# Layer 0's depthwise convolution split between VectorE and TensorE, and zeros only in the border cells of layer 1's table

## The chip, the cores and the metric

The kernel runs on one core of one Trainium2 chip. Time is the device time of one execution, in microseconds (us). In all that follows PE is TensorE (PEld its weight loads), DVE is VectorE, ACT is ScalarE, POOL is GpSimd and SP is SyncE, which only issues transfers here. All data is fp32 unless said otherwise.

## What is computed

The reference is a network of four layers on an input x of 2 images, 64 x 64 positions and 128 channels. Only its first two steps concern the change:

```
# layer 0, for each image: x = x + f(groupnorm(x)), and f begins
xz   = h @ W_in.T                   # 128 -> 512: 256 channels xs, 256 channels z
xs   = silu(depthwise_conv3x3(xs))  # each channel with nine weights of its own, zero padding
...                                 # four selective scans over xs, layernorm, gate silu(z), W_out
# layer 1: x = x + deformable_conv3x3(groupnorm(x))
#   reads the image at computed positions, four neighbours each; outside the image a neighbour counts as 0
```

Layer 2 (a selective scan with 512 channels and 256 states, then spectral filters) and layer 3 (attention, then a mixture of experts) are unchanged and follow after that.

## The kernel before, in words

The input X (128 partitions x 64 tiles x 128 channels, 4.2 MB) is loaded whole with eight transfers of 512 KB on SP's queue (`move`, L1353). Before that, `zero_table` fills layer 1's table with zeros by one transfer on POOL's queue (L437). The table lies in DRAM: for each of the two images 67 x 67 cells of 512 values (2 KB), 18.4 MB in all. A cell holds the values of four neighbouring positions, so that layer 1 can fetch all four with one gather (L534). Layer 1 itself writes the cells that belong to image positions with sixteen transfers (L480), long after layer 0.

`layer0` goes through the two images one after the other, and each image through three blocks:

- The block before the scan. The 32 tiles of the image are transposed to channels on partitions (`to_channels`, L95, copies L72 and L74, into xt, 128 x 4096). `groupnorm` takes statistics on DVE (L132, L133), sums them over groups of channels by matmuls with the constant gmat (pm L136, pq L143; gmat is loaded on SP's queue behind X, L200), and normalises xt in place (L146). Then PE forms z (pz, L209, 16 matmuls), ACT applies Silu and SP stores z to DRAM (L211, L212). For each half h of the 256 channels, PE forms px (L221, 8 matmuls of 128 x 512), which DVE and ACT copy in turn into the middle of xp, a tile of 66 x 66 with a frame of zeros. The convolution is done on PE: for each of eight pieces q of 8 image rows, nine matmuls (L227) of the diagonal matrix `dw[:, h * 9 + t]` with the shifted window of xp are added up in PSUM (pc), and ACT writes Silu of it to U (L228). The 18 diagonal matrices are products of the identity with a column of weights, made by DVE (L215).
- The scan (L255 to L394), an order written out by hand. It begins with copies of U to uc (L255).
- The block after the scan: layernorm, gate, W_out, and the sum onto X (L403 to L425).

Outside the scan a scheduler orders the instructions of each engine by their dependences; an engine then works through its own list in that order. Constants of layer 0 (w_xp L170, w_dt L172, w_out L179; sel L175 and L177, mean_w L181, an L183 and L184, dd L187) are loaded or made within the first block of the first image. PSUM has six buffers for the tiles of the first block, and the working pool `wk` has three of each of its tiles.

Of the kernel before, what the change touches and what calls it, by code (L numbers as in the profile page):

```python
# [16 lines left out]
F32 = mybir.dt.float32  # L17
# [3 lines left out]
ALU = mybir.AluOpType  # L21
# [4 lines left out]
P = 128  # L26
B, HH, WW, C = 2, 64, 64, 128
# [13 lines left out]
TS = 67  # L41
# [48 lines left out]
def to_channels(k, ps, out, tile_of, n):  # L90

    for g in range(0, n, 4):
        pt = ps.tile([P, N], F32, name="pt", tag="ps")
        for j in range(4):
            k.nc.tensor.transpose(pt[:, j * P : (j + 1) * P], tile_of(g + j), k.ident)  # L95
        k.copy(out[:, g * P : (g + 4) * P], pt)
# [29 lines left out]
def groupnorm(k, pool, ps, gmat, xt, tag):  # L126

    nc = k.nc
    st = pool.tile([P, 8, 6], F32, name=f"{tag}_st", tag=f"{tag}_st")
    mv = pool.tile([P, 2], F32, name=f"{tag}_mv", tag=f"{tag}_mv")  # L130
    for i in range(8):
        nc.vector.bn_stats(st[:, i, :], xt[:, i * N : (i + 1) * N])  # L132
    nc.vector.bn_aggr(mv, st.rearrange("p a b -> p (a b)"))  # L133
    mg = pool.tile([P, 1], F32, name=f"{tag}_mg", tag=f"{tag}_mg")
    pm = ps.tile([P, N], F32, name="pm", tag="ps")
    nc.tensor.matmul(pm[:, 0:1], gmat, mv[:, 0:1], start=True, stop=True)  # L136
    nc.vector.tensor_copy(mg, pm[:, 0:1])
    q = pool.tile([P, 1], F32, name=f"{tag}_q", tag=f"{tag}_q")
    nc.vector.tensor_tensor(q, mv[:, 0:1], mg, ALU.subtract)
    nc.vector.tensor_tensor(q, q, q, ALU.mult)  # L140
    nc.vector.tensor_tensor(q, q, mv[:, 1:2], ALU.add)
    pq = ps.tile([P, N], F32, name="pq", tag="ps")
    nc.tensor.matmul(pq[:, 0:1], gmat, q, start=True, stop=True)  # L143
    rs = pool.tile([P, 1], F32, name=f"{tag}_rs", tag=f"{tag}_rs")
    rsqrt(nc, pool, rs, pq[:, 0:1], 1e-5, [P, 1], tag)
    nc.vector.tensor_scalar(xt, xt, mg, rs, ALU.subtract, ALU.mult)  # L146


def zero_frame(nc, t):

    nc.gpsimd.memset(t[:, 0, :], 0.0)
    nc.gpsimd.memset(t[:, 65, :], 0.0)
    nc.gpsimd.memset(t[:, 1:65, 0:1], 0.0)
    nc.gpsimd.memset(t[:, 1:65, 65:66], 0.0)
# [4 lines left out]
def layer0(k):  # L159
    tc, nc, ins, X = k.tc, k.nc, k.ins, k.X  # L160
    T = N
    NC = L // T
    with ExitStack() as es:
# [29 lines left out]
        for b in range(B):  # L193
            Xb = X[:, b * NTB : (b + 1) * NTB, :]
            with ExitStack() as e2:
                pre = e2.enter_context(tc.tile_pool(name=f"l0p{b}", bufs=1))
                wk = e2.enter_context(tc.tile_pool(name=f"l0w{b}", bufs=3))
                ps = e2.enter_context(tc.tile_pool(name=f"l0ps{b}", bufs=6, space=PSUM))
                gmat = pre.tile([P, P], F32, name="gmat")
                nc.sync.dma_start(out=gmat, in_=ins["gmat"])  # L200
                w_in = pre.tile([P, 512], F32, name="w_in")
                nc.sync.dma_start(out=w_in, in_=ins["w_in0"])
                xt = pre.tile([P, L], F32, name="xt")
                to_channels(k, ps, xt, lambda i: Xb[:, i, :], NTB)
                groupnorm(k, pre, ps, gmat, xt, "gn")
                for h in range(2):
                    for q in range(8):
                        pz = ps.tile([P, N], F32, name="pz", tag="ps")
                        nc.tensor.matmul(pz, w_in[:, 256 + h * P : 256 + (h + 1) * P], xt[:, q * N : (q + 1) * N], start=True, stop=True)  # L209
                        z = wk.tile([P, N], F32, name="z")  # L210
                        nc.scalar.activation(z, pz, AF.Silu)  # L211
                        nc.sync.dma_start(out=zs[h, :, b * L + q * N : b * L + (q + 1) * N], in_=z)  # L212
                dw = pre.tile([P, 18, P], F32, name="dw")
                for j in range(18):
                    nc.vector.tensor_scalar(dw[:, j, :], k.ident, k.v("conv_w")[:, j : j + 1], None, ALU.mult)  # L215
                for h in range(2):
                    xp = pre.tile([P, 66, 66], F32, name="xp", bufs=2)
                    zero_frame(nc, xp)
                    for q in range(8):
                        px = ps.tile([P, N], F32, name="px", tag="ps")  # L220
                        nc.tensor.matmul(px, w_in[:, h * P : (h + 1) * P], xt[:, q * N : (q + 1) * N], start=True, stop=True)  # L221
                        k.copy(xp[:, 1 + 8 * q : 9 + 8 * q, 1:65], px.rearrange("p (h w) -> p h w", w=WW))
                    for q in range(8):
                        pc = ps.tile([P, N], F32, name="pc", tag="ps")
                        for t in range(9):
                            ky, kx = divmod(t, 3)
                            nc.tensor.matmul(pc, dw[:, h * 9 + t, :], xp[:, 8 * q + ky : 8 * q + ky + 8, kx : kx + WW], start=t == 0, stop=t == 8)  # L227
                        nc.scalar.activation(U[:, h, q * N : (q + 1) * N], pc, AF.Silu, bias=k.v("conv_b")[:, h : h + 1])  # L228

            with ExitStack() as e2:  # L230
                ch = e2.enter_context(tc.tile_pool(name=f"l0h{b}", bufs=2))
                sm = e2.enter_context(tc.tile_pool(name=f"l0s{b}", bufs=1))
                wk = e2.enter_context(tc.tile_pool(name=f"l0k{b}", bufs=3))
# [77 lines left out]
                at = lambda i: (todo[i][0], NC - 1 - todo[i][1] if todo[i][0] >= 2 else todo[i][1])  # L311
# [4 lines left out]
                def spread(bc, q):  # L316
                    br = wk.tile([P, 4, T], F32, name="br", bufs=2)
                    nc.sync.dma_start(out=br, in_=bc[4 * q : 4 * q + 4, :].partition_broadcast(P))
                    return br

                def c_row(cs, n):
                    o = pc_.tile([P, T], F32, name="pcn")
                    nc.tensor.matmul(o, sel[:, n, :], cs, start=True, stop=True)  # L323
                    return o
# [13 lines left out]
                with tc.manual_schedule():  # L338
                    rows, pcn, last, save = spread(ready[0][1], 0), c_row(ready[0][2], 0), None, None
                    for it, (kk, ci) in enumerate(todo):  # L340
                        c = at(it)[1]
                        uc, bc, cs, dt, du, ea = ready.pop()
                        f = T - 1 if kk >= 2 else 0
# [6 lines left out]
                        for n in range(16):  # L350
# [13 lines left out]
                            flat, dflat = (t.rearrange("p h t -> p (h t)")[:, s_] for t in (S, dA))  # L364
# [23 lines left out]
                            if n % 4 == 2:  # L388
                                if n < 14:
                                    rows = spread(bc, n // 4 + 1)  # L390
                                elif ready:
                                    rows = spread(ready[0][1], 0)
# [4 lines left out]
            with ExitStack() as e2:  # L397
                wk = e2.enter_context(tc.tile_pool(name=f"l0f{b}", bufs=2))
# [30 lines left out]

def zero_table(k, pool, table):  # L430

    nc = k.nc
    row = B * TS * 4
    z = pool.tile([P, row], F32, name="zero")
    nc.gpsimd.memset(z, 0.0)
    flat = table.rearrange("a c -> (a c)").rearrange("(p g f) -> p g f", p=P, f=row)
    nc.gpsimd.dma_start(out=flat, in_=z.unsqueeze(1).to_broadcast([P, TS, row]))  # L437


def layer1(k, table):  # L440
# [915 lines left out]
def kernel(tc, ins, out, stages=STAGES):  # L1356
    nc = tc.nc
    with ExitStack() as es:
# [8 lines left out]
        if two or "0" in stages or "1" in stages:  # L1367
            with tc.tile_pool(name="x01", bufs=1) as xp:
                k.X = xp.tile([P, NT, C], F32, name="X")
                move(nc, k.X, tokens(x))  # L1370
                if "1" in stages:
                    table = dr.tile([B * TS * TS, 4 * C], F32, name="table")
                    with tc.tile_pool(name="zt", bufs=1) as zp:
                        zero_table(k, zp, table)
                if "0" in stages:
                    layer0(k)
                with ExitStack() as e2:
                    if two:
                        mix = mixing_weights(k, dr, e2)
                    if "1" in stages:  # L1380
                        layer1(k, table)
                    if two:
                        weights = mix()
                if two:
                    norm_tokens(k, rs, sh)
                x = dr.tile([B * L, C], F32, name="x1")
                move(nc, tokens(x), k.X)
# [119 lines left out]
```

## Time and profile before

| | |
|---|---|
| median of 3 runs | 16111.0 us (16098.64 to 16113.83) |
| the profiled execution | 16122.4 us, its span 16120.6 us |
| mean granted TensorE clock | 0.902 |
| busy share of the span | PE 76%, PEld 45%, DVE 86%, ACT 61%, POOL 84% |
| first matmul of the convolution, image 1 and 2 | 92.25 us and about 2402 us |
| last Silu of the convolution, image 1 and 2 | 222.93 us and 2533.5 us |
| layer 1: first table store, first gather | 4700.6 us and 4873.8 us |

The profiled execution is one execution on the chip. A line of the profile's groups gives the source line, engine, operation, and output and inputs by the names of the program, then the count, and after the bar the busy time in us, the mean duration of one in ns, and the idle time of the engine just before them with what ended it. Each fp32 matmul appears as two records, one for each pass. A line of waits gives who waited for whom, the total in us, how often, and the longest. A line of windows gives the stretch in us, its length, the busy time and number of instructions of each engine, the granted TensorE clock as a share of full speed, the mean busy share of the 16 DMA engines, and the GB/s moved. A line of the timeline gives the start in us, the time to the end of the last of the instructions merged in it, and their number.

### The profile page before, as it was taken

The numbers are of one execution on the slowest core, as the hardware profiler recorded it, in microseconds if no ns is written. First come the engines' busy times: TensorE is split into PE (matmuls) and PEld (weight loads), VectorE is DVE, ScalarE is ACT, GpSimd is POOL, SyncE is SP. The second block draws the span as 40 slices with busy tenths as digits, with TensorE's granted clock in tenths as the row PEclk, the third lists the DMA queues.
The fourth block names the chain that finished last, engine by engine and source line by source line (L and its number), as shares of the span: only waits on it lengthen the run. The fifth ranks groups of instructions, "written<-read, shape, count | busy, mean of one in ns | idle before, by whom it ended". The sixth has DMA issues, their size and how long they took to land.

```text
span 16120.6 us, 190989 instructions
## 1 busy us (share of the span) xinstructions
PE 12236.8 (76%) x69886; PEld 7246.4 (45%) x69886; DVE 13783.2 (86%) x12003; ACT 9835.0 (61%) x15912; POOL 13463.0 (84%) x5125
## 2 busy tenths in 40 slices
PE   6666657666667864549778679879788888888897
PEld 2222223222227851325445446546445555555565
DVE  4999975999964359999999999999999999999973
ACT  3666634666610027777777677777777777777752
POOL 3888835888817879999999999999999999999970
PEclk8999989999988876769889889989999999999998
DMA  2111111111135544546555556556666665565543
GB/s 102 69 71 69 68 51 49 70 71 69 69 93 160 160 143 151 168 150 203 183 187 195 174 181 199 193 184 203 192 193 198 189 204 195 190 205 194 188 169 128
DMA packets 1214859, 2389.69 MB, mean 148 GB/s; under 512 B 346648, under 2 KB 923288, under 8 KB 1047904
## 3 DMA queue, kind: packets, MB, share of 16 engines
q1 hardware_dynamic: 1162672, 2206.74, 41.7%
q0 software_dynamic: 50384, 169.42, 3.5%
q8 instruction: 552, 9.04, 0.2%
q14 instruction: 387, 3.17, 0.1%
q10 hardware_dynamic: 864, 1.32, 0.0%
HBM read 2018.49 MB, written 358.65 MB: 147 GB/s over the span
## 4 chain that ended last, share of the span: by engine, by line
POOL 34%; PE 13%; DVE 10%; DMA 3%; ACT 2%; issue 1%; SPq 0%; POOLq 0%; ACTq 0%; DVEq 0%
POOL S L1082 33%; DVE S L1138 10%; PE pef L966 6%; PE Z L1100 2%; PE acc L939 2%; DMA row<-drow 2%; PE pw L765 1%; POOL S L1088 1%; ACT ze L1106 1%; ACT dA L1136 0%; DMA w<-in_w_b_dram 0%; DMA w<-in_w_delta_dram 0%; ACT e L946 0%; PE acc L1001 0%; DMA e<-mdr 0%
## 5 line engine op out<-in xcount | busy, mean ns | idle before, releaser
L1138 DVE TENSOR_TENSOR_SCAN S<-dA,S 128x512 f32<-128x512 f32 x8192 | 9226.5, 1200 | 393.0 <-ACT dA L1136 208.4
L1082 POOL TENSOR_TENSOR S<-row,g 128x4096 f32<-128x4096 f32 x1024 | 9103.0, 8895 | 256.3 <-DMA row<-drow 219.8
L1136 ACT ACTIVATE dA<-row,a_t 128x512 f32<-128x512 f32 x8192 | 5614.4, 692 | 2146.0 <-DVE S L1138 2107.7
L1100 PE MATMUL Z<-S,cv 128*32 128x256 f32 x32768 | 2499.4, 435 | 1494.0 <-ACT ze L1106 1240.3
L966 PE MATMUL pef<-hk,ur 128*128 128x256 f32 x14336 | 3512.1, 388 | 138.8 <-ACT e L946 120.0
L966 PEld LDWEIGHTS pef<-hk,ur 128*128 128x128 f32 x14336 | 2644.6, 191 | 1077.6 <-issue 563.4
L365 DVE TENSOR_TENSOR_SCAN S<-dA,S 128x1024 f32<-128x1024 f32 x1024 | 2339.1, 2284 | 243.7 <-ACT dA L363 96.8
L354 POOL TENSOR_TENSOR S<-du,br 128x1024 f32<-128x1024 f32 x1024 | 2410.3, 2357 | 138.6 <-DVE M L379 83.3
L1100 PEld LDWEIGHTS Z<-S,cv 128*32 128x32 f32 x32768 | 999.9, 121 | 2698.6 <-issue 1289.2
L394 PE MATMUL yp<-M,ident 128*128 128x512 f32 x4096 | 2062.6, 627 | 2.9 <-DVE M L379 2.9
L394 PEld LDWEIGHTS yp<-M,ident 128*128 128x128 f32 x4096 | 821.7, 201 | 2091.7 <-issue 2052.7
L363 ACT ACTIVATE dA<-dt,an 128x511 f32<-128x511 f32 x2048 | 1406.9, 687 | 209.0 <-DVE S L365 132.0
L379 DVE TENSOR_TENSOR M<-S,pcn 128x1024 f32<-128x1024 f32 x1024 | 1250.5, 1221 | 110.5 <-DVE S L365 6.9
L323 PE MATMUL pcn<-cs,sel 80*128 80x512 bf16 x1024 | 409.3, 400 | 1180.4 <-DVE M L379 1169.8
L1106 ACT COPY ze<-Z 128x512 f32<-128x512 f32 x1024 | 1122.4, 1096 | 235.0 <-PE Z L1100 201.2
L939 PE MATMUL acc<-e,mw 128*128 128x512 f32 x1920 | 1042.2, 631 | 29.1 <-ACT e L946 28.5
L534 POOL DMA_INDIRECT G<-table,idx x576 | 802.2, 1393 | 261.1 <-issue 175.1
L966 PEld LDWEIGHTS pef<-hd,ur 128*128 128x128 f32 x4096 | 761.4, 195 | 491.7 <-issue 233.0
L966 PE MATMUL pef<-hd,ur 128*128 128x256 f32 (+1 forms) x4096 | 882.0, 342 | 99.8 <-ACT e L946 93.8
L541 DVE TENSOR_TENSOR V<-G,wt 128x4608 f32<-128x4608 f32 x64 | 317.5, 4962 | 609.0 <-DMA G<-table,idx 590.9
L367 ACT COPY stt<-S 128x2 f32<-128x2 f32 x896 | 168.9, 189 | 1083.5 <-DVE S L365 1080.3
L553 PE MATMUL pv<-ident,V 128*128 128x128 f32 x4608 | 615.3, 302 | 52.1 <-issue 48.8
(323 smaller groups left out, 8302.1 us busy)
## 6 DMA issues: line engine op xcount, KB each, us to landing
row<-drow SPq DMA_DIRECT2D x1024, 1024.0 KB
br<-bc SPq DMA_DIRECT2D x256, 1024.0 KB
zd<-ze SPq DMA_DIRECT2D x1024, 256.0 KB
hk<-in_phi_dram SPq DMA_DIRECT2D x128, 576.5 KB
hk<-in_phi_dram SPq DMA_DIRECT2D x96, 704.5 KB
hd<-in_phi_dram SPq DMA_DIRECT2D x512, 128.5 KB
mw<-wdr SPq DMA_DIRECT2D x480, 128.0 KB
hk<-in_phi_dram SPq DMA_DIRECT2D x160, 320.5 KB
```

The source lines that it names most:

```text
L354: nc.gpsimd.tensor_tensor(S, du, br[:, n % 4, :].unsqueeze(1).to_broadcast([P, 2, T]), ALU.mult)
L363: nc.scalar.activation(dA[:, h, rest], dt[:, h, rest], AF.Exp, scale=an[:, kk * 2 + h, n : n + 1])
L365: nc.vector.tensor_tensor_scan(flat, dflat, flat, 0.0, ALU.mult, ALU.add)
L379: nc.vector.tensor_tensor(M, S, pcn.unsqueeze(1).to_broadcast([P, 2, T]), ALU.mult)
L394: nc.tensor.matmul(yp[:, h, :], k.ident, M[:, h, :], start=False, stop=n == 15)
L939: nc.tensor.matmul(acc.rearrange("p a s -> p (a s)"), ms[f][:, o, :], e, start=box["first"], stop="whole" in box and (f, o) == todo[-1])
L966: nc.tensor.matmul(pe[:, a, 256 - n :], ur[:, par, j, :], h[:, at : at + n], start=i == 0, stop=i + 1 == len(mm))
L1082: nc.gpsimd.tensor_tensor(S, row.unsqueeze(1).to_broadcast([P, 2, R, T]), g.unsqueeze(2).to_broadcast([P, 2, R, T]), ALU.mult)
L1100: nc.tensor.matmul(Z[32 * j : 32 * j + 32, q], cv[:, h, s], S[:, h, :, s], start=h == 0, stop=h == 1)
L1106: nc.scalar.copy(ze.rearrange("p q t e -> p q e t"), Z)
L1136: nc.scalar.activation(dA, row[:, j % R, :], AF.Exp, scale=a_t[:, h, d : d + 1])
L1138: nc.vector.tensor_tensor_scan(s, dA, s, 0.0, ALU.mult, ALU.add)
```

## The change

The convolution's nine taps are divided. Taps 0, 1 and 2 (the upper row of the 3 x 3 window) stay as matmuls with diagonal matrices. Taps 3 to 8 are added up by DVE in a tile sv: one tensor_scalar (window times weight), then five scalar_tensor_tensor (window times weight, plus sv, in place). PE adds sv to pc by a matmul with the identity. So PE does four matmuls for a piece q instead of nine, and DVE six instructions that it did not have. Only six diagonal matrices per image are left, and POOL makes them. The tile dw shrinks from 18 to 6 matrices of 512 bytes per partition; three buffers of sv, 2 KB per partition each, are added.

`zero_table` now writes zeros only where layer 1 writes no or not all values of a cell: for each image the first two and last two rows of cells (two transfers of 2 x 67 cells), and in between, for each row, the last two cells together with the first two of the next row (one transfer of 64 pieces of 8 KB). These are six transfers, 2.15 MB in all, instead of one of 18.4 MB.

The scheduler's lists differ only around these parts: in DVE's list the sv instructions of neighbouring pieces q are interleaved, and the making of sel, mean_w, an and dd stands before the first copies of px; in ACT's list the exponential for an stands before the first z, one table load less is needed, and three of the first four copies to uc stand before the last Silu of the convolution; in SP's list w_xp, w_dt and w_out stand before the stores of z; in POOL's list three of the products dw stand between the first four and the last two transfers of zeros, the other three after them.

```diff
@@ layer0
-                dw = pre.tile([P, 18, P], F32, name="dw")
-                for j in range(18):
-                    nc.vector.tensor_scalar(dw[:, j, :], k.ident, k.v("conv_w")[:, j : j + 1], None, ALU.mult)
+                KT = 3
+                dw = pre.tile([P, 2, KT, P], F32, name="dw")
+                for h in range(2):
+                    for t in range(KT):
+                        nc.gpsimd.tensor_scalar(dw[:, h, t, :], k.ident, k.v("conv_w")[:, h * 9 + t : h * 9 + t + 1], None, ALU.mult)
...
                     for q in range(8):
+                        tap = lambda t: xp[:, 8 * q + t // 3 : 8 * q + t // 3 + 8, t % 3 : t % 3 + WW]
+                        cw = lambda t: k.v("conv_w")[:, h * 9 + t : h * 9 + t + 1]
+                        sv = wk.tile([P, 8, WW], F32, name="sv")
+                        nc.vector.tensor_scalar(sv, tap(KT), cw(KT), None, ALU.mult)
+                        for t in range(KT + 1, 9):
+                            nc.vector.scalar_tensor_tensor(sv, tap(t), cw(t), sv, ALU.mult, ALU.add)
                         pc = ps.tile([P, N], F32, name="pc", tag="ps")
-                        for t in range(9):
-                            ky, kx = divmod(t, 3)
-                            nc.tensor.matmul(pc, dw[:, h * 9 + t, :], xp[:, 8 * q + ky : 8 * q + ky + 8, kx : kx + WW], start=t == 0, stop=t == 8)
+                        for t in range(KT):
+                            nc.tensor.matmul(pc, dw[:, h, t, :], tap(t), start=t == 0, stop=False)
+                        nc.tensor.matmul(pc, k.ident, sv.rearrange("p a b -> p (a b)"), start=False, stop=True)
@@ zero_table
-    row = B * TS * 4
-    z = pool.tile([P, row], F32, name="zero")
+    z = pool.tile([P, 4 * 4 * C], F32, name="zero")
     nc.gpsimd.memset(z, 0.0)
-    flat = table.rearrange("a c -> (a c)").rearrange("(p g f) -> p g f", p=P, f=row)
-    nc.gpsimd.dma_start(out=flat, in_=z.unsqueeze(1).to_broadcast([P, TS, row]))
+    flat = table.rearrange("a c -> (a c)")
+    cell = 4 * C
+    for b in range(B):
+        at = b * TS * TS * cell
+        for y in (0, TS - 2):
+            rows = flat[at + y * TS * cell : at + (y + 2) * TS * cell].rearrange("(p f) -> p f", p=P)
+            nc.gpsimd.dma_start(out=rows, in_=z[:, : 2 * TS * cell // P])
+        edge = flat[at + (TS + TS - 2) * cell :]
+        dst = bass.AP(edge.tensor, edge.offset, [[TS * cell, TS - 3], [1, 4 * cell]])
+        nc.gpsimd.dma_start(out=dst, in_=z[: TS - 3, :])
```

## The prediction

> **What bounds the kernel now.** I read the windows by stage first, then inside layer 0 the waits, the groups and the timeline, then the DMA view of the first 100 us. The page's chain of waits is of no use here: it reaches back only to about 5846 us, and no line of layer 0 is in it. The layers follow one another through X, so whatever shortens a stage of layer 0 in which nothing else runs should shorten the whole.
>
> By stage (busy us and count for PE, PEld, DVE, ACT, POOL, then TensorE clock, DMA share, GB/s):
>
> ```profile
> 0.00:92.25 92.25, 31.74 (x85) 17.57 (x85) 20.58 (x47) 17.61 (x27) 5.25 (x16) 0.69 0.81 304
> 92.25:223.50 131.25, 130.64 (x305) 57.25 (x303) 9.20 (x19) 16.69 (x24) 0.00 (x0) 1.00 0.00 1
> ...
> 2402.00:2534.00 132.00, 131.43 (x307) 57.56 (x305) 3.47 (x5) 13.78 (x21) 0.00 (x0) 1.00 0.00 0
> ```
>
> The two long rows are the convolutions of the two images: PE is busy all the time at full clock, while DVE, ACT, POOL and the DMA engines have next to nothing to do. The first row is the opposite: PE is two thirds idle and the DMA engines are 81% busy.
>
> The waits from 60 to 230 us (total, times, longest), and the groups of the first convolution:
>
> ```profile
> ACT U L228 <- PE pc L227: 109.9, 16, 7.1
> DVE xp L72 <- PE px L221: 79.8, 8, 56.2
> ...
> PE pm L136 <- DMA gmat<-in_gmat_dram: 25.5, 1, 25.5
> ```
>
> ```profile
> L227 PE MATMUL pc<-xp,dw 128*128 128x512 f32 x288 | 123.9, 592 | 0.0
> ```
>
> ACT and DVE wait for PE, so PE's 144 tap matmuls (288 records, two passes each) set the stage: 123.9/144 = 0.86 us each. Ahead of that, PE waits for gmat, 64 KB, until 62.97 us. The DMA view of 0 to 100 us says why:
>
> ```profile
> q0 software_dynamic: 4304, 18.39, 44.6%
> q1 hardware_dynamic: 11760, 9.71, 30.2%
> ...
> table<-zero POOLq DMA_DIRECT2D x1, 17956.0 KB
> X<-in_x_dram SPq DMA_DIRECT2D x8, 512.0 KB
> ```
>
> The zeros of layer 1's table, 18.39 MB, travel beside X (4.2 MB), and gmat stands behind X in SP's queue. From 8 to 60 us the engines move some 410 GB/s, so they are full. The X waits and gmat are one queue that the zeros slow down.
>
> **What the Trainium skill says.** "DMA: Bandwidth & Descriptors", section "Issuing engines are not separate DMA queues": transfers of all issuers run on the same 16 engines and interleave. The trace agrees: q0 and q1 together stay at 410 GB/s. "TensorE: Matmul & The Clock Gate", section "What's actually happening": PE runs at half clock after idling and at full clock after a few busy us. It agrees: the clock is 0.50 from 40 to 60 us, pz's passes are 0.85 us apart until 73.6 us and 0.43 after. "VectorE: DVE Perf Modes", section "The perf-mode tier table": an fp32 tensor_scalar in SBUF runs at twice the rate of an fp32 tensor_tensor. It agrees (L86 and L87 below, 0.43 and 0.69 us). The same page's section "The DRAIN you can't avoid" says the next op starts when the pipeline is empty, with an exception for ops that aren't held; here independent ops start before their predecessor ends:
>
> ```profile
> 2297.76 0.43 DVE L86 TENSOR_SCALAR yn_s<-yn_s 128x512 f32<-128x512 f32 x1
> 2298.22 0.69 DVE L87 TENSOR_TENSOR rs<-rs,yn_s 128x512 f32<-128x512 f32 x1
> 2298.95 1.42 DVE L418 SCALAR_TENSOR_TENSOR Y<-Y,pv,rs 128x512 f32<-128x512 f32 x2
> 2300.28 1.41 DVE L419 SCALAR_TENSOR_TENSOR Y<-Y,pv,zt 128x512 f32<-128x512 f32 x2
> ```
>
> L418 lasts 0.749 us, yet two take 1.33 us from start to start of L419: 0.665 us each. A dependent op (L86 to L87) starts its predecessor's duration plus 0.03 us later.
>
> **Part 1, the taps, on PE.** Per half h (two halves per image, four in all) PE had 8 px and 72 tap matmuls, 80 x 0.86 = 68.8 us; from px to px in the trace it is 154.06 - 85.38 = 68.68. Now it has 8 px, 24 taps and 8 sv, 40 x 0.86 = 34.4 us.
>
> **On DVE.** Per half it gets 8 tensor_scalar and 40 scalar_tensor_tensor beside its 4 copies of px. In the changed instruction order the chains of two q run interleaved, so the op waited for is nearly always the one before the last. I price each scalar_tensor_tensor at 0.665 us, a tensor_scalar at 0.35 (0.43 less the same overlap of 0.08), a copy at 0.61 (0.69 less 0.08): 40 x 0.665 + 8 x 0.35 + 4 x 0.61 = 31.8, and 0.5 for the few dependent pairs, at each half's end above all: 32.3 us. The copies come every 1.72 us (two px), and sv work fills the gaps. Bounds: with every op dependent and the tensor_scalar at single rate, 40 x 0.78 + 8 x 0.69 + 4 x 0.69 = 39.5; below 32.3 I see no reason to go but give 31. The rows that these ops read lie 66 apart; copies of px into the same tile cost 0.694 us against 0.690 into a flat one, so I price that at nothing.
>
> **Put together.** The px of the second half stand behind the last sv matmul on PE, and DVE's first copy behind the first px: 0.1 + 0.86 + 1.06 (px start to copy start, 85.38 to 86.44) = 2.0 us without DVE work. 32.3 + 2.0 = 34.3, PE alone 34.4: both are full, each waiting for the other now and then (PE for the first sv about 0.6 us, then for an sv every 3.7 us where it needs 3.4). I take 35.3 us per half, with 34.4 and 42 as the ends. Saved: 4 x (68.68 - 35.3) = **133.5 us** (107 to 137).
>
> New waits: PE's sv matmul waits for DVE, and behind it the next taps and px are queued; that is the 1 us above. The third sv buffer is waited for by the tensor_scalar of q + 3, whose release (PE's matmul of q) comes more than one q earlier. ACT's U waits as before, for less. DVE's work on sel, mean_w, an and dd (6.6 us) now stands before the px copies; it falls under pz, where DVE idles 17.37 us. ACT's load and exponential for an (1.28 + 0.31 us) move between L82 and the first z; ACT is free 4.3 us there, so nothing. One table load goes (1.28 us, was hidden).
>
> **Part 2, dw.** 18 products on DVE become 6 on POOL, per image. DVE's were under waits for X (first image) and PE (second: L425 started at 2362.14, right at the end of PE's po). POOL's are not in the trace; a 128x128 of it can hardly cost more than its 16x512 at 1.15 us, so at most 7 us. POOL idles until 227 us, and in the second image from 2359 to past 2500 with dw needed at about 2402. Nothing, either way.
>
> **Part 3, the zeros.** Six transfers of 2 x (2 x 274 + 524) KB = 2.15 MB replace 18.39 MB. 8.58 MB had moved by 25 us and 23.2 MB by 63 us, with gmat last. Now some 7 MB must move up to gmat: at 0.41 MB/us that is reached 1.6/0.41 = 4 us before 25 us, at 21; X's 512-byte pieces alone moved at 347 GB/s in the later load of X (15793 us), which makes it 23. With the end of gmat's own transfer PE's pm starts at 24 instead of 62.97: **39 us** saved. The four X pieces of the first image and DVE's statistics after them (5.9 us in the trace) are done by about 21. Ends: 31 saved if the start-up stretch (125 to 300 GB/s up to 8 us) lasts longer, 42 if not. The last two zero transfers wait on POOL for the first four, with dw queued behind: a few us, needed at 53 at the earliest. DVE's sel, ACT's an and SP's w_xp now wait for all six; they stand after L146, L82 and w_in, at 24 us or later, when the zeros should have landed by 20. SP's three weight loads move ahead of the zs stores: 1.2 us of issue and 0.7 MB, in the idle stretch before z.
>
> **Part 4, the hand-over.** Three of the four uc copies now stand before the last U on ACT: 0.9 us per image, 1.8.
>
> Sum: 133.5 + 39 + 1.8 = 174.3 us. The profiled execution took 16122.4 us (span 16120.6); the median of the runs is 11.4 lower, 16111.0. From the median: **15937 us**. A measurement of this kernel tells about 0.2%, 32 us, from no change.
>
> **The rivals.**
> A. DVE becomes the bound, its ops costing their full length (the 39.5 us above, 41.5 per half): 4 x 27.2 = 109 saved, with the start 150: 15961. For it: sv is updated in place. Against it: the interleaved order, and L418's 0.665.
> B. PE, now waiting for DVE in every q, falls to half clock: 40 x 1.71 = 68.4 us per half, nothing won there; the start and the hand-over alone leave 16111 - 40.8 = 16070. Against it: the scan loop of layer 0 keeps PE busy 1313.6 of 1950 us and its clock at 0.95; here gaps are under 1 us.
> C. The start gains little, since X itself is slow: 15 us instead of 39, 15961. For it: 8192 pieces of 512 bytes; against it: the 347 GB/s.
> D. Slower: the strided scalar_tensor_tensor starts anew on each row of 64 and takes over three times its flat length, so that DVE bounds the stage at more than PE did. The start and the hand-over give 40.8 us, 10.2 per half, so it decides from (68.68 + 10.2 - 7.2)/40 = 1.8 us per op on (7.2 being copies, tensor_scalars and the 2.0); at 2.2 us a half takes 95.2, and 4 x 26.5 - 40.8 = 65 us are lost: 16176. Against it: the strided copies' 0.694 us.
> E. The change not doing what it says: the order of instructions shows the taps moved and the six transfers, so only the waits could undo it.
>
> **How the numbers follow.** Forecast 0.70, A 0.14, C 0.08, B 0.05, D 0.03. The forecast's own ends are 15925 and 15965; with A, C and the spread of runs (15 us) the range is 15905 to 15980, leaving out B, D and some of the tails. Faster by over 0.2%: all but D and a small part of B, 0.96; within 0.2%: 0.02; slower: 0.02.
>
> **What would show it.** Right: pm starting at about 24 us; from px to px of the two halves 35 us; scalar_tensor_tensor starts 0.67 us apart; PEclk 1.00 there; the time from the first U to layer 1 otherwise unchanged. Wrong: pm after 32 us, halves above 40 us, a clock of 0.5 in the convolution, or a gap on ACT between L82 and z.

## The result and the profile after

The change made the kernel faster by 1.1%: 15931.2 us median of four runs (15925.6 to 15935.8) against 16112.4 of four runs of the kernel before (16098.6 to 16122.8), a ratio of 0.9888 with a 95% interval of 0.9871 to 0.9905. The profiled execution took 15934.9 us, its span 15933.1. So 181 us went by the medians, and 187.5 by the two profiled spans (16120.6 - 15933.1).

The windows of the kernel after, one for the start and one for each half of the two convolutions (stretch, its length, busy us and count of PE, PEld, DVE, ACT, POOL, then TensorE clock, DMA share, GB/s):

```profile
0.00:47.30 47.30, 25.25 (x68) 14.71 (x69) 18.71 (x39) 16.46 (x25) 10.36 (x27) 1.00 0.70 232
47.30:82.11 34.81, 34.81 (x81) 14.83 (x80) 32.52 (x52) 8.14 (x13) 0.00 (x0) 1.00 0.07 26
82.11:117.50 35.39, 34.97 (x81) 14.63 (x79) 32.52 (x52) 9.17 (x16) 0.00 (x0) 1.00 0.00 0
2287.07:2321.88 34.81, 34.81 (x82) 14.83 (x81) 32.52 (x52) 8.21 (x13) 0.00 (x0) 1.00 0.07 26
2321.88:2357.60 35.72, 34.96 (x81) 14.63 (x79) 32.51 (x52) 9.52 (x17) 0.00 (x0) 1.00 0.00 1
```

Each half takes half as long as before (34.81 us from px to px, 68.68 before), and PE and DVE are both nearly full in it: PE 34.81 of 34.81 us, DVE 32.52. PE is still the bound, by a little. The first px came at 85.38 us and now comes at 47.30. The clock of 1.00 in the first row is not a reading for the whole row, since the clock records of this trace begin at 36.5 us; a second trace of the same kernel ("after, again" below) has 0.78 in that stretch.

The waits of the first convolution, 47 to 119 us (total, times, longest):

```profile
ACT U L237 <- PE pc L236: 43.8, 15, 3.7
...
DVE xp L72 <- PE px L224: 13.4, 2, 11.3
...
PEld pc L236 <- DVE sv L232: 7.4, 16, 0.8
```

The groups of the same stretch:

```profile
L232 DVE SCALAR_TENSOR_TENSOR sv<-xp,pv,sv 128x512 f32<-128x512 f32 x80 | 55.1, 748 | 0.2
L235 PE MATMUL pc<-xp,dw 128*128 128x512 f32 x96 | 43.8, 592 | 0.0
...
L236 PE MATMUL pc<-sv,ident 128*128 128x512 f32 x32 | 16.9, 611 | 0.0
...
L230 DVE TENSOR_SCALAR sv<-xp,pv 128x512 f32<-128x512 f32 x16 | 7.7, 483 | 0.2
```

DVE's 11.3 us of waiting lie before the first px; between the halves it waits 2.1 us. Only PE's weight loads wait for sv, at most 0.8 us; the matmuls themselves have no idle time (the last 0.0 of L235 and L236). The start of the kernel in PE's timeline:

```profile
13.93 3.68 PE L95 MATMUL pt<-ident,X 128*128 128x128 f32 x16 [2.12 <-DMA X<-in_x_dram]
24.50 0.56 PE L136 MATMUL pm<-gn_mv,gmat 128*128 128x1 f32 x2 [6.90 <-DMA gmat<-in_gmat_dram]
...
30.49 16.98 PE L209 MATMUL pz<-xt,w_in 128*128 128x512 f32 x32 [3.94 <-issue]
47.30 3.17 PE L224 MATMUL px<-xt,w_in 128*128 128x512 f32 x7
```

The DMA view of 0 to 100 us, two queues (packets, MB, share of the 16 engines) and the transfers of zeros (KB each):

```profile
q1 hardware_dynamic: 11760, 9.71, 29.7%
q0 software_dynamic: 480, 2.15, 5.9%
...
table<-zero POOLq DMA_DIRECT2D x4, 268.0 KB
table<-zero POOLq DMA_DIRECT2D x2, 512.0 KB
```

POOL's queue moves 2.15 MB instead of 18.39. PE still waits for gmat, but 6.9 us instead of 25.5, and pm starts at 24.50 instead of 62.97.

**Where the 187.5 us went**, by points that both traces have: 38.1 up to the first px; 68.33 and 68.34 from first px to first pd (the matmul that begins the scan) of the two images (138.89 to 70.56, 138.89 to 70.55); together 174.8. The scans and the blocks after them gave 5.4 more, so that layer 1's first table store came 180.2 us earlier (4700.65 to 4520.48). The remaining 7 us fell in layers 1 to 3, whose code is the same. From the table store to layer 3's load of X (15791.47 and 15599.36) the kernel before took 11090.8 us, the one after 11078.9, and the ten other executions below 11079.9 to 11108.4. A difference of this size there can't be put down to the change, and **layer 1's first table store is a better yardstick** for a change in layer 0 than the whole time. It isn't free of this either: the two scans with the blocks after them, whose code is the same in all twelve traces, took 4330.6 to 4338.3 us together (4337.5 before, 4332.1 after), so that the 5.4 us are not shown to come from the change, and a few us at the store say little. The start and the two convolutions alone, which gave 174.8 us, are the sharpest measure.

### The profile page after: what moved, and what is told of

It reads as the page before. It is cut to its first block, busy times and chain, and to the rows that moved or that the text cites. A ratio compares the mean times of both kernels' runs of the same rounds, so it can differ in the third digit from the quotient of the medians.

```text
span 15933.1 us, 190559 instructions
## 1 busy us (share of the span) xinstructions
PE 12090.7 (76%) x69566; PEld 7172.8 (45%) x69566; DVE 13888.6 (87%) x12159; ACT 9835.1 (62%) x15911; POOL 13460.0 (84%) x5142
## 4 chain that ended last, share of the span: by engine, by line
POOL 42%; DVE 16%; PE 14%; issue 6%; DMA 3%; ACT 3%; SPq 0%; POOLq 0%; DVEq 0%; ACTq 0%
POOL S L1101 36%; DVE S L1157 9%; PE pef L985 5%; DVE S L374 5%; POOL G L553 4%; DMA row<-drow 2%; PE Z L1119 2%; PE acc L958 2%; PE yp L403 1%; DVE M L388 1%; PE pw L784 1%; PE po L505 1%; POOL S L363 1%; POOL S L1107 1%; ACT ze L1125 0%
## 5 line engine op out<-in xcount | busy, mean ns | idle before, releaser
L553 POOL DMA_INDIRECT G<-table,idx x576 | 795.9, 1382 | 261.1 <-issue 174.8
```

The lines of the kernel that those rows point to most:

```text
L553: nc.gpsimd.indirect_dma_start(out=G[:, o, :], out_offset=None, in_=table, in_offset=bass.IndirectOffsetOnAxis(ap=idx[:, t * 9 + o : t * 9 ...
```

## The experiments

Ten experiments ran, on three chips; nine are other kernels, and "after, again" is the kernel after itself. The ratio of each is to runs of the kernel before on its own chip (medians 16121.4, 16120.0 and 16117.1). "After, again" ran on the chip of "mixed"; on the chips of the other eight the kernel after has no run recorded beside them. Times in us; "px to pd" is the first convolution, "store" the first table store. The second convolution took the same within 0.3 us, but for taps only.

| kernel | median | ratio to before, 95% | first px | px to pd | store |
|---|---|---|---|---|---|
| before | 16112.4 | | 85.38 | 138.89 | 4700.65 |
| after | 15931.2 | 0.9888 (0.9871 to 0.9905) | 47.30 | 70.56 | 4520.48 |
| taps only | 15978.5 | 0.9909 (0.9893 to 0.9926) | 86.14 | 78.37 | 4569.52 |
| zeros only | 16089.7 | 0.9981 (0.9973 to 0.9988) | 54.09 | 138.88 | 4662.49 |
| two taps on PE | 15966.1 | 0.9905 (0.9888 to 0.9922) | 47.92 | 79.67 | 4544.71 |
| four taps on PE | 15963.5 | 0.9904 (0.9888 to 0.9921) | 47.20 | 83.53 | 4547.42 |
| gmat first | 16110.9 | 0.9992 (0.9983 to 1.0000) | 72.37 | 138.88 | 4684.56 |
| one chain | 15959.4 | 0.9902 (0.9885 to 0.9918) | 48.34 | 77.94 | 4538.62 |
| sum from pc | 15962.9 | 0.9900 (0.9884 to 0.9917) | 42.82 | 75.64 | 4531.72 |
| share for POOL | 15978.4 | 0.9910 (0.9894 to 0.9927) | 43.33 | 83.55 | 4549.00 |
| mixed | 15944.6 | 0.9892 (0.9876 to 0.9909) | 43.69 | 73.90 | 4526.98 |
| after, again | 15934.7 | 0.9887 (0.9870 to 0.9903) | 47.52 | 70.56 | 4520.17 |

### The two parts alone

Taps only (after with the old zeros), and zeros only (before with the new zeros); both edits are shown against the kernel after, with most of their lines left out:

```diff
 # taps only: zero_table of before put back
-    for b in range(B):
...
+    nc.gpsimd.dma_start(out=flat, in_=z.unsqueeze(1).to_broadcast([P, TS, row]))
 # zeros only: layer0 of before put back, nine taps on PE
...
-                        nc.vector.scalar_tensor_tensor(sv, tap(t), cw(t), sv, ALU.mult, ALU.add)
+                            nc.tensor.matmul(pc, dw[:, h * 9 + t, :], xp[:, 8 * q + ky : 8 * q + ky + 8, kx : kx + WW], start=t == 0, stop=t == 8)
```

> Only the split of the taps, with the one 18.4 MB transfer of zeros as before. Theory (two independent gains, the convolution's and the start's): PE's pm stays at about 63 us, from px to px of the two halves 34.8 us as with the whole change, so 4 x (68.7 - 34.8) = 136 and 2 at the hand-over are saved: 15973 us. Rival (the convolution owes part of its gain to the free DMA engines, or the exponential for an, now ahead of z on ACT and waiting for all zeros, holds z back): halves above 36 us, or px later than 22.8 us after pm; 15980 to 16000.

> Only the border zeros, with all nine taps on PE as before. Theory: pm at 24.5 us instead of 63, everything after it as before and 38 us earlier: 16073 us. Rival (what is won at the start is given back, as the convolution or z then meets the transfers): the first px no more than 20 us earlier, 16090.

Measured: the taps alone bring 143 us by the medians, 131.1 at the table store; the zeros alone 32 and 38.2. The signs and sizes are those of the prediction's parts. Two details are not.

With the zeros alone, pm starts at 25.71, near the forecast, but the first px gains only 31.3 us and not 38. DVE's timeline of that kernel shows why:

```profile
28.63 0.16 DVE L84 TENSOR_TENSOR gn_s<-gn_rs 128x1 f32<-128x1 f32 x1
29.14 0.91 DVE L175 MEMSET sel<- 80x1024 uint32 x1 [0.36 <-issue]
...
33.92 1.65 DVE L187 TENSOR_SCALAR dd<-ident,pv 128x128 f32<-128x128 f32 x8
35.49 0.15 DVE L85 TENSOR_TENSOR gn_s<-gn_s,gn_v 128x1 f32<-128x1 f32 x1
```

The scheduler put the constants (sel, mean_w, an, dd), 6.35 us, between two steps of the group norm's square root, L84 and L85. Everything waits behind them: L146, which normalises xt, starts at 36.05, and pz at 38.57 instead of 30.49. In the kernel after, by DVE's timeline, the same constants stand behind L146 and lie under pz, where DVE is idle:

```profile
27.20 0.16 DVE L84 TENSOR_TENSOR gn_s<-gn_rs 128x1 f32<-128x1 f32 x1
27.40 0.16 DVE L85 TENSOR_TENSOR gn_s<-gn_s,gn_v 128x1 f32<-128x1 f32 x1
...
27.98 2.41 DVE L146 TENSOR_SCALAR xt<-xt,gn_mg,gn_rs 128x4096 f32<-128x4096 f32 x1
30.54 0.91 DVE L175 MEMSET sel<- 80x1024 uint32 x1 [0.16 <-issue]
```

In the kernel before, too, they stood elsewhere, behind the first copies of px. From pm to px the kernel with the zeros alone takes 28.4 us, against 22.4 before and 22.8 after. So of the 6.8 us that it lacks at the first px some 6 belong to this order of DVE's list and the rest to the later pm; the smaller transfers gave what was expected of them. Why the scheduler chose that place was not looked into. Likewise, with the taps alone it set the second half's px of image 1 between the taps of the first half; that convolution took 78.37 us, 7.8 more than in the kernel after, while image 2, with px in one block as there, took 70.55. By the first px and the two convolutions the two parts alone make 128.1 + 31.3 = 159.4 us of the 174.8, and the missing 15 are these two orders; at the store they make 169.3 of the 180.2, since with the zeros alone the scans and the blocks after them took 4330.6 us, the least of the twelve traces.

### Two and four taps on PE

```diff
-                KT = 3
+                KT = 2    # the other kernel: KT = 4
```

> The whole change with two taps on PE and seven on DVE. Theory (both engines are full at three taps): PE falls to 32 x 0.86 = 27.5 us per half, DVE rises to 8 x 0.40 + 48 x 0.66 + 4 x 0.61 = 37.3 us, so DVE sets the half with 2 us of hand-over, 39.5: 4 x 4.7 = 19 us slower than the whole change, 15950. Rival (PE alone bounds it, DVE has room): halves of 28 to 31 us, 15905.

> The whole change with four taps on PE and five on DVE. Theory: PE 48 x 0.86 = 41.3 us per half and nearly never waiting, 41.5: 4 x 6.7 = 27 us slower than the whole change, 15958. Rival (DVE's chain is the bound, PE only waits for it): DVE falls by 5.3 us per half, and so do the halves, to 30 us, 15910.

Measured from px to pd: 79.67 with two taps and 83.53 with four, against 70.56 with three, that is +4.6 and +6.5 us per half (4.7 and 6.7 were expected). With four, a half has 8 more PE matmuls (6.9 us), px to px is 41.20, and DVE waits for PE. The window of the first half with four taps, in the columns used above:

```profile
47.20:88.40 41.20, 41.20 (x97) 18.18 (x96) 28.92 (x44) 8.15 (x13) 0.00 (x0) 1.00 0.06 22
```

With two, PE waits for DVE. A window of that kernel's first convolution, where DVE is the full one:

```profile
72.21:90.00 17.79, 14.44 (x30) 4.84 (x29) 17.79 (x30) 4.61 (x9) 0.00 (x0) 1.00 0.00 0
```

And from its waits, 47 to 128 us:

```profile
PE pc L236 <- DVE sv L232: 13.1, 8, 4.1
```

The bound changes sides between two and three taps, and both steps have about the size of the work that was added to the engine named. Three taps give the shortest time of the three divisions. In the two-tap kernel the mean clock was also 0.75 in the window from 90 to 127 us, where PE works 24.72 of 37.00 us and waits up to 4.1 us at a time: what the prediction's rival B feared is seen there, late in the stage, and not in the kernel after, whose windows of the convolution show 1.00. That the waits alone brought the clock down was not tested.

### The order of DVE's sums

The kernel after with the convolution's order written out by hand, each piece's six instructions in a row:

```diff
+                    with tc.manual_schedule():
                     for q in range(8):
```

> The whole change, but the pieces q in the order written: on DVE the six sv instructions of one q run in a row, each waiting for the one before. Theory (a dependent op costs its full length and 0.03 us, an independent one 0.66): 40 x 0.78 + 8 x 0.51 + 4 x 0.61 = 37.7 us on DVE, halves of 39.7, 20 us slower than the whole change, 15951. Rival (DVE drains between ops in any order, the interleaving is worth nothing): scalar_tensor_tensor starts as far apart as before, halves of 34.8, 15931.

Measured: px to pd 77.94, 7.4 us more per image, with 37.6 us from px to px where 39.7 was expected; store 18.1 later. DVE's timeline of this kernel:

```profile
60.88 3.97 DVE L233 SCALAR_TENSOR_TENSOR sv<-xp,pv,sv 128x512 f32<-128x512 f32 x5
64.76 0.48 DVE L231 TENSOR_SCALAR sv<-xp,pv 128x512 f32<-128x512 f32 x1
```

DVE's timeline of the kernel after:

```profile
60.23 0.48 DVE L230 TENSOR_SCALAR sv<-xp,pv 128x512 f32<-128x512 f32 x1
60.62 4.06 DVE L232 SCALAR_TENSOR_TENSOR sv<-xp,pv,sv 128x512 f32<-128x512 f32 x6
64.60 0.48 DVE L230 TENSOR_SCALAR sv<-xp,pv 128x512 f32<-128x512 f32 x1
```

In a row, five take 64.76 - 60.88 = 3.88 us from start to start, 0.776 each; interleaved, six take 3.98, 0.663 each. The edit fixes the order of PE and ACT too, but DVE's instructions follow each other without a gap in the lines above, so its own spacing sets the pace. The interleaving that the scheduler found is worth about 15 us over both images; the other order has the mechanism of rival A, at less than half of A's price.

### gmat ahead of X

The kernel before, with gmat and w_in of the first image loaded ahead of X:

```diff
+                nc.sync.dma_start(out=k.early[0], in_=ins["gmat"])
+                nc.sync.dma_start(out=k.early[1], in_=ins["w_in0"])
                 move(nc, k.X, tokens(x))
```

> The kernel before, with gmat and w_in of the first image loaded ahead of X on SP's queue; 18.4 MB of zeros stay. It tells gmat's place in the queue from the bytes in flight. Theory (the bytes decide: X's pieces and SP's list behind them are slow, whatever stands first): pm starts when DVE's statistics end, at about 42 us instead of 63, but SP can issue the stores of z only after its eight pieces of X, at 56 us, and z has three buffers, so the first px comes at 70 to 76 instead of 85.4: 10 to 15 us faster, 16099. Rival (only gmat's place mattered): px 21 us earlier, at 64, 16090; or more.

Measured: first px at 72.37, 13.0 us earlier, within the forecast, and no change that the times can tell (16110.9, interval of the ratio up to 1.0). SP's timeline of that kernel shows what then holds the start:

```profile
2.60 53.71 SPq L1356 DMA_DIRECT2D X<-in_x_dram  x8
56.42 19.38 SPq L215 DMA_DIRECT2D zs<-z  x16
```

And ACT's timeline:

```profile
63.91 1.88 ACT L214 ACTIVATE z<-pz 128x512 f32<-128x512 f32 x3 [7.56 <-DMA zs<-z]
```

X's own issue lasts until 56 us beside the zeros, z's stores stand behind it, and ACT waits for its three z buffers. With the run of the zeros alone, this says that the bytes of the zeros cost the 38 us; an earlier gmat alone gets back a third.

### Attempts at a faster version

Sum from pc: gmat first; px copied by ACT alone; DVE starts the sum from pc in PSUM, so that the tensor_scalar and the identity matmul go. Share for POOL: as that, with piece q = 4 of each half summed by POOL. Mixed: as the first, but pieces 0 and 1 of each half keep the tensor_scalar and the identity matmul.

```diff
-                        nc.vector.tensor_scalar(sv, tap(KT), cw(KT), None, ALU.mult)
+                            nc.vector.scalar_tensor_tensor(sv, tap(KT), cw(KT), pc.rearrange("p (a b) -> p a b", b=WW), ALU.mult, ALU.add)
-                        nc.tensor.matmul(pc, k.ident, sv.rearrange("p a b -> p (a b)"), start=False, stop=True)
 # share for POOL, for q = 4:
+                                nc.gpsimd.tensor_scalar(tm, tap(t), cw(t), None, ALU.mult)
+                                nc.gpsimd.tensor_tensor(sv, sv, tm, ALU.add)
 # mixed: the first three lines only where not alone
+                        alone = q < 2
```

> The whole change, with gmat and w_in of the first image ahead of X, the px copies all on ACT, and DVE's sum starting from pc: the first op is scalar_tensor_tensor with pc from PSUM, the identity matmul goes, and ACT reads sv for U. PE has 32 x 0.86 = 27.5 us per half, DVE 48 x 0.66 = 31.7. Theory (two full engines; taking work from both shortens the half): 32 to 33 us, as DVE now never waits for px; 4 x 2.3 = 9, and 3.5 at the start: 15918. Rival (DVE now waits for PE at each q, and PE for DVE at the change of halves): 35 us or more, 15928 or later.

> As the kernel with the sum starting from pc, but piece q = 4 of each half is summed by POOL (six products, five sums) and added by PE with the identity. DVE has 42 x 0.66 = 27.7 us per half, PE 33 x 0.86 = 28.4, POOL 11 ops of 1.2 to 1.6 us, 15 us. Theory: halves of 29 us, 4 x 5.8 + 3.5 = 27 us faster than the whole change, 15904. Rival (POOL and DVE hinder each other at SBUF, or POOL's op takes over 2.5 us): DVE's scalar_tensor_tensor lasts longer than 0.75 us while POOL works, or PE waits for POOL's sum; halves of 33 us or more, 15918 or later.

> What three taps with a separate sum leave on the table: the loads of the group norm's matrix and of the input weights stand ahead of the image's load for image 1 (4.5 us at the start in the kernel whose sum began from PSUM), all copies of px go to ACT, and only the first two of a half's eight pieces are summed apart and joined by the identity matmul, so that VectorE has work while TensorE is at its first taps; the other six start from pc in PSUM and need no identity matmul. Loads of a half worked out from the traces: TensorE 8 x 0.86 (px) + 24 x 0.86 (taps) + 2 x 0.86 (identity) = 29.2 us instead of 34.4; VectorE 2 x (0.40 + 5 x 0.66) + 6 x 6 x 0.66 = 31.2 us, the new bound. Theory (the larger of the two engines' loads, and the first half's wait): from first px to pd of image 1 some 2 + 62.4 + 2 = 66.5 us instead of 70.6, a first px at 42.8, and with the second image 2 x 4 + 4.5 = 12.5 us in the trace: 15922 beside an after of 15934 on this chip, some 0.1%. Rival (the wait of the kernel whose sum began from PSUM comes back, since VectorE reaches the third piece before TensorE does, which is held by the second piece's identity matmul): first px to pd 72 to 76 us, and no gain or a loss of a few us.

> The changed kernel itself, on the same chip as the mixed one, for a comparison of like with like: 15931 (15920 to 15945) if chips agree as closely as its runs did; first px to pd of image 1 70.6 us as before. What it leaves over the kernels whose sum began from PSUM (15963 on another chip) tells how much of their loss was the chip: under 5 us of drift by both theories.

None beat the kernel after. The earlier gmat did bring some 4 us (first px at 42.82, 43.33 and 43.69). The convolutions lost more: 10.2, 26.2 and 6.7 us over both images.

Sum from pc missed its 15918 and came to 15962.9. DVE can't start before eight px and three taps are through PE, 9.7 us after the first px, against 1.1 in the kernel after. Its timeline has it:

```profile
52.55 0.75 DVE L247 SCALAR_TENSOR_TENSOR sv<-xp,pv,pc 128x512 f32<-128x512 f32 x1 [18.65 <-PE pc L236]
```

PE's timeline at the end of the same convolution:

```profile
118.46 3.78 PE L281 MATMUL pd<-uc,w_xp 128*128 128x512 f32 x4 [20.54 <-ACT uc L277]
```

From 52.55 us on DVE runs without a gap, 96 x 0.66 us, some 63 us, while PE has finished long before, waits 20.5 us and does pd at 0.95 us a pass instead of 0.5. "TensorE: Matmul & The Clock Gate" of the Trainium skill, section "What's actually happening", tells of half clock after idling, and this pair of numbers agrees, as does the granted clock of 0.50 from 118.46 to 122.24 us. By the start and the convolutions this kernel is 5.7 us behind the kernel after, at the store 11.2, the rest of that in the scans, whose code is the same; the rest of its distance lies in layers 1 to 3, which took 11108.4 us in this execution, the most of all.

The share for POOL missed its 15904 by more. The groups of 43 to 128 us without POOL's share (sum from pc):

```profile
L249 DVE SCALAR_TENSOR_TENSOR sv<-xp,pv,sv 128x512 f32<-128x512 f32 x80 | 54.7, 742 | 0.3
...
L247 DVE SCALAR_TENSOR_TENSOR sv<-xp,pv,pc 128x512 f32<-128x512 f32 x16 | 11.8, 737 | 18.7 <-PE pc L236 18.7
```

The same groups with POOL's share:

```profile
L249 DVE SCALAR_TENSOR_TENSOR sv<-xp,pv,sv 128x512 f32<-128x512 f32 x70 | 59.1, 900 | 0.5
...
L243 POOL TENSOR_SCALAR tm<-xp,pv 128x512 f32<-128x512 f32 x10 | 18.2, 1820 | 0.8
L244 POOL TENSOR_TENSOR sp<-sp,tm 128x512 f32<-128x512 f32 x10 | 14.1, 1414 | 0.8
...
L247 DVE SCALAR_TENSOR_TENSOR sv<-xp,pv,pc 128x512 f32<-128x512 f32 x14 | 10.4, 741 | 23.1 <-PE pc L236 23.1
```

DVE has ten instructions fewer on L249, yet more busy time: 900 ns each instead of 742. The form with pc, one of whose two tensors is in PSUM, stays at 741. "GPSIMD Engine Reference" of the Trainium skill, section "1. Specifications", says that POOL and DVE share SBUF interfaces and contend where the DVE instruction has two SBUF inputs (or runs in a two-port mode); the two rows agree with just that distinction.

The mean of 900 hides two cases. The 40 instructions of L249 that run while POOL is idle take 0.73 to 0.75 us. Of the 30 beside POOL, 15 take no longer, six take 1.06 to 1.18, all begun inside a tensor_scalar of POOL, and nine take 1.57 to 1.76. Each of these nine starts inside a tensor_tensor of POOL and ends 0.55 us after it, as in this timeline:

```profile
54.78 1.79 POOL L244 TENSOR_TENSOR sp<-sp,tm 128x512 f32<-128x512 f32 x1
...
55.55 1.57 DVE L249 SCALAR_TENSOR_TENSOR sv<-xp,pv,sv 128x512 f32<-128x512 f32 x1
```

So DVE is not slowed evenly: by these nine pairs its two-input instruction is held until POOL's tensor_tensor is over. The rival's other half came true as well: PE waits for POOL's sum, and behind it the taps of the next pieces. From the waits of this kernel, 43 to 128 us:

```profile
PE pc L245 <- POOL sp L244: 10.3, 2, 6.4
```

DVE in turn waits 4.0 us more for these pc (1.4 us in the first half, 2.6 in the second). Its busy time from the first px to pd is 3.6 us longer than without POOL's share (67.8 and 64.2), in spite of the fewer instructions. The two together are 7.6 of the 7.9 us by which this convolution is longer.

Mixed came to 15944.6 beside 15934.7 for the kernel after on the same chip (15938.6 to 15948.3, and 15927.6 to 15943.7), and 6.8 us later at the store (4526.98 and 4520.17). By the start and the convolutions it is 2.9 us behind; the rest fell in the scans and in layers 1 to 3, whose code is the same. The rival was right in size (72 to 76 us from px to pd, measured 73.9), not in its reason. DVE had done the first two pieces by 53 us and then waited 7.0 us for the third pc, in its timeline:

```profile
60.20 0.75 DVE L241 SCALAR_TENSOR_TENSOR sv<-xp,pv,pc 128x512 f32<-128x512 f32 x1 [7.00 <-PE pc L235]
```

PE's timeline of that kernel, up to that pc's taps:

```profile
50.55 2.74 PE L235 MATMUL pc<-xp,dw 128*128 128x512 f32 x6
53.13 1.02 PE L245 MATMUL pc<-sv,ident 128*128 128x512 f32 x2
53.99 2.74 PE L235 MATMUL pc<-xp,dw 128*128 128x512 f32 x6
56.56 1.02 PE L245 MATMUL pc<-sv,ident 128*128 128x512 f32 x2
```

PE was not held by anything. It works through px and taps without a gap from 43.69 on, and just needs until 60 us for eight px, nine taps and two identity matmuls. The two identity matmuls are 1.7 us of the 7.0. A sum that starts on PE puts PE's whole lead into DVE's wait; a sum that starts apart, as in the change, lets both engines begin with px.

## Why the prediction was right

It said 15937 us; the median is 15931.2. Its sum was 174.3 us, and the landmarks it spoke of moved by 174.8, its three terms being off by -0.9, +2.0 and -0.6 us (measured less forecast), which partly cancel. By its steps:

- **The start, 39 us forecast:** pm moved by 38.5 us (24.50, forecast 24), the first px by 38.1. Of its two rates the slower one held: from 5 to 25 us the engines moved 336 GB/s on average (256 to 388), near its 347 and not its 410. That DVE's list leaves L146 undisturbed, as the order of instructions said, is worth some 6 us; zeros only showed it.
- **The convolution, 4 x (68.68 - 35.3) = 133.5:** a half takes 34.81, so this is 135.5. The mis-sized term is the 1 us for PE's waits on sv: a half is 80 passes of 0.43, 34.4, and only 0.4 more. DVE's 32.3 was 32.5: scalar_tensor_tensor 0.66 from start to start (0.665 forecast), tensor_scalar 0.40 (0.35 forecast). The 2.0 us between halves without DVE work were 2.1.
- **The hand-over, 1.8:** from the last pc to pd 0.6 us less per image (1.37 to 0.78), so 1.2.
- **dw on POOL, nothing:** each took some 0.6 us where up to 1.15 was allowed for. The first image's last three waited for POOL's turn after the zeros and were done by 15.6 us, needed at 54. POOL waited 4.5 us for the first zeros, and nobody for POOL.
- **The constants and ACT's list, nothing:** DVE's constants ended at 37.0, before px at 47.3; ACT's first z started at 32.57, 2.1 us after the first pz. So it was.
- **Rivals:** A is the one-chain kernel, though its price was too high: in that order a half took 37.6 us, not 41.5. B fell (clock 1.00). C fell at 38.1 us. D fell at 0.748 us, with windows whose rows lie 66 apart.
- **The ends:** those of its terms add up to 15930 (137 + 42 + 1.8 saved) and 15971 (107 + 31 + 1.8), not to its 15925 and 15965. Its range holds both.

The mechanism was right, and every term within 2 us. What it did not have is the 13 us beyond 174.8 in the spans, all of them in scans and layers that are unchanged, where executions differ by as much. That the median still lies within 6 us of its figure is in that part luck: the medians moved by 181 us.

## What to carry to other kernels

Where one engine is full and another idle in a stage with nothing beside it, count both engines' loads per step for each division and take the one where they meet; then look at who starts first, since a chain that begins on the slow side's output gives the gain back as a wait. A transfer that nobody waits for still costs by its bytes whatever stands behind it on the same DMA engines. And look at what a scheduler does with the engine's list around the edit: here it moved 6 us at the start and 7.8 us in a convolution in or out of the path.

## What was not expected of the hardware

- An elementwise instruction of POOL at 128 x 512 fp32 took 1.41 us (tensor_tensor) and 1.82 us (tensor_scalar) on average in the kernel with a share for POOL, beside DVE's 0.69 and 0.48. Nine of the ten tensor_tensors in its first convolution held one DVE instruction with two SBUF inputs until they were over; the form with one input in PSUM kept its 0.74 us.
- scalar_tensor_tensor depends on its neighbours: 0.776 us from start to start if it needs the one before (one chain), 0.663 if not (the kernel after).
- Unchanged layers of 11.09 ms differed by up to 29 us between executions (11078.9 to 11108.4). The cause was not looked for and stays open.
